# Stage 1 of a chain of weight products by six 64-column products instead of seven, and half of a side computation one iteration later

## The chip, the cores and the metric

The kernel runs on one core of a Trainium2 chip. Its time is the device time of one launch in microseconds (us); lower is better. Three runs of the kernel before gave 474.98, 475.28 and 476.53 us.

## What is computed

128 samples of 64 channels by 1024 positions pass through four modulated 1-D convolutions ("same", "upsample" with a blur behind it, "same", "downsample" with a blur ahead of it), and the input is added to the result. Each sample has weights of its own: a style vector scales the weights by input channel, and they are normalised by output channel.

```python
def _layer(x, style, w, b, mw, mb, typ):
    s = style @ mw.T + mb
    weight = SCALE * w * s[:, None, :, None]
    demod = lax.rsqrt(jnp.sum(weight * weight, axis=(2, 3)) + EPS)
    weight = weight * demod[:, :, None, None]
    ...
    elif typ == 'upsample':
        out = jax.vmap(_conv_up)(x, weight.transpose(0, 2, 1, 3)) + b[None, :, None]
        out = _blur(out, 2.0 * blur_k, (1, 1))
    ...
for i, typ in enumerate(TYPES):
    out = _layer(out, style, weights[i], biases[i], mod_w[i], mod_b[i], typ)
x = x + out
```

There is no nonlinearity between the layers, so the four layers of one sample are one linear map. The kernel first multiplies the weights of the layers together, sample by sample, and then convolves the input once with the merged weights.

## The kernel before

Samples go in fours: `q` runs from 0 to 31, and iteration `q` handles four samples, two in each half of the 128 partitions. Every matrix product works on 64x64 blocks, and four of them (two halves of the rows, two halves of the columns) stand together as one group; each of these is fp32 and appears as two instructions in the profile, so one group gives eight MATMUL instructions.

The chain of weights of a group of samples has three stages.

- **Stage 1** multiplies the last layer's three taps with the third layer's three taps. That is a product of two polynomials with three coefficients each, whose result has five blocks of 64 columns. For the first samples, and for one group more, `stage1` does it directly with nine block products. For the other 28 groups `scale3` (ScalarE) writes the last layer's taps w0, w1, w2, scaled, and the sums w0+w1 and w1+w2 (five blocks, copied from `w3x`), `stage1_a` issues three tap products into the PSUM tile `psS` and ScalarE evicts four blocks of it to the SBUF tile `S`; `stage1_b` issues two more tap products on top of what stands in PSUM, and VectorE's SCALAR_TENSOR_TENSOR (line 481) evicts those sums to `S` while it subtracts a block that ScalarE evicted. GpSimd adds two blocks of `S` (line 484). In block products this is 2+2+1 in `stage1_a` and 1+1 in `stage1_b`, seven in all. The weights of these products are `w2n`, the third layer's taps negated and their sums.
- **Stage 2** multiplies `S` with the nine blurred taps `E` into `psR`. Where `sharing(q)` holds (iterations 5 to 27), `share_sums` (VectorE, line 501) forms sums of blocks of `S` one iteration ahead, `share` multiplies them (TensorE) into unused columns of `psA`, `share_copy` (ScalarE, line 529) copies those to `psR`, and `stage2_rest` adds the rest.
- **Stage 3** multiplies the result `R` with the first layer's taps into `W`, from which VectorE forms the combinations `H`.

The convolution (`product`, line 803) streams 340 columns per MATMUL: `conv3`, `conv1`, `conv2` and `conv0` accumulate in `psA`, `conv4` in `Y`. VectorE forms their inputs `T` from the samples `X` through `G` (`in_g2`, `in_g01` at line 712, `in04` at line 790, `in3` at line 761), GpSimd forms two of them (lines 776 and 781), and `sum1` and `sum2` on VectorE carry partial sums; `conv4` of an iteration waits for `sum2`.

The order of instructions on each engine is written out by hand: `early_turn` for iterations 0 to 3, `turn_of` for 4 to 28, and the last ones apart. `psS` and `psR` share one buffer (`ps_w` has one), so `share_copy` can write only when VectorE's eviction of `S` has read `psS`. The rows' ends are computed apart from the convolution, and that work is put into single iterations by the tables `SIDE`, `LATE` and `SLOTS`: `side(SIDE, q)` stands on VectorE between `in_g2` and the eviction of `S`, `side(LATE, q)` after `in3`. `setup1(0)` and `setup1(1)` blur the second layer's taps for the row ends, two VectorE instructions each; `ends1`, a product in iteration 14, reads their result.

## Time and profile before

| what | before |
|---|---|
| runs (us) | 474.98, 475.28, 476.53; median 475.28 |
| the profiled execution: its span (us), the one time that the profile gives for it | 475.5 |
| granted TensorE clock, mean | 0.998 |
| TensorE busy (us, share of the span) | 469.7 (99%) |
| VectorE busy | 417.3 (88%) |
| ScalarE busy | 312.0 (66%) |
| GpSimd busy | 165.8 (35%) |
| data moved, mean rate | 70.71 MB, 149 GB/s |

The page lists, for each engine, the time in which it was busy. PE is TensorE's matmuls, PEld its weight loads, DVE VectorE, ACT ScalarE, POOL GpSimd, SP the queue that issues most DMAs. In the timeline each row is a run of like instructions: the start in us, the time from the first start to the last end, the engine, the line of the kernel, the operation, the tiles written and read, the shapes and the count, and in brackets the engine's idle time before it with what ended it. Because matmuls overlap, the time that a run of them takes of the engine is read from its start to the start of the next run.

### The profile page before, as it was taken

What the parts mean: (1) busy time and instruction counts of PE and PEld (TensorE: products, weight loads), DVE (VectorE), ACT (ScalarE), POOL (GpSimd) and SP (SyncE); (2) the same over time, 40 slices, a digit from 0 to 9 for tenths busy, and PEclk for the clock granted to TensorE, in tenths of its full rate; (3) what the DMA queues carried; (4) which work ended last, traced back from release to release, by engine and by line L of the source; (5) the groups of instructions that cost most, each with busy time, mean ns of one, the idle gap of its engine ahead of it and who ended that gap; (6) DMA issues with size and microseconds to landing.
All of it is one profiled execution on the core that took longest, in us unless ns stands there. A gap on an engine that the chain in (4) does not pass through costs nothing.

```text
span 475.5 us, 26771 instructions
## 1 busy us (share of the span) xinstructions
PE 469.7 (99%) x11932; PEld 349.5 (74%) x11932; DVE 417.3 (88%) x694; ACT 312.0 (66%) x711; POOL 165.8 (35%) x200
## 2 busy tenths in 40 slices
PE   9999999999999999999999999999999999999996
PEld 6987788777678876677776677766788787876653
DVE  3889998879989998899979899979998999999896
ACT  4565657577766676766667666667666777766464
POOL 3634033664444342233432233422333423243200
PEclk9999999999999999999999999999999999999999
DMA  5237456535445554345544454543555544455225
GB/s 176 71 115 224 150 151 180 152 113 177 139 145 166 166 166 136 123 150 169 163 150 126 130 168 152 178 124 121 152 164 169 164 145 147 148 152 161 80 91 193
DMA packets 52707, 70.71 MB, mean 149 GB/s; under 512 B 6000, under 2 KB 50672, under 8 KB 52592
## 3 DMA queue, kind: packets, MB, share of 16 engines
q1 hardware_dynamic: 52368, 68.78, 46.3%
q8 instruction: 93, 1.52, 1.4%
q10 hardware_dynamic: 224, 0.22, 0.1%
q14 instruction: 22, 0.18, 0.1%
HBM read 35.36 MB, written 33.62 MB: 145 GB/s over the span
## 4 chain that ended last, share of the span: by engine, by line
PE 99%; DVE 0%; ACT 0%; issue 0%
PE psA L803 47%; PE Y L803 12%; PE psR L506 9%; PE psW L621 7%; PE psA L621 7%; PE psS L428 6%; PE psR L589 5%; PE psA L506 2%; PE Y L1044 2%; PE Y L183 1%; PE Y L379 1%; PE psM L220 0%; PE psE L1044 0%; PE Y L255 0%; DVE o L882 0%; PE psM L255 0%
## 5 line engine op out<-in xcount | busy, mean ns | idle before, releaser
L803 PE MATMUL psA<-T,H 64*64 64x340 f32 x2304 | 185.9, 446 | 0.0
L803 PEld LDWEIGHTS psA<-T,H 64*64 64x64 f32 x2304 | 90.7, 133 | 46.9 <-issue 2.5
L712 DVE SCALAR_TENSOR_TENSOR G<-X 128x1376 f32<-128x1376 f32 (+2 forms) x65 | 78.0, 1206 | 0.2
L776 POOL TENSOR_TENSOR T<-G 128x684 f32<-128x684 f32 x28 | 46.3, 1652 | 73.7 <-DVE G L712 73.7
L484 POOL TENSOR_TENSOR S<-S 128x128 f32<-128x128 f32 x28 | 21.6, 772 | 139.7 <-ACT S L399 139.6
L399 ACT ACTIVATE R<-psR,tC 128x448 f32<-128x448 f32 x63 | 36.6, 631 | 43.6 <-PE psR L506 25.8
L803 PE MATMUL psA<-T,Wf 64*64 64x340 f32 x768 | 63.7, 446 | 0.0
L803 PE MATMUL Y<-T,Wf 64*64 64x340 f32 x768 | 62.4, 451 | 0.0
L712 DVE SCALAR_TENSOR_TENSOR Y<-m,psA 128x340 f32<-128x340 f32 x62 | 32.0, 516 | 28.2 <-PE psA L803 26.9
L399 ACT ACTIVATE psW<-psA 128x128 f32<-128x128 f32 x100 | 19.3, 268 | 49.1 <-PE psA L621 45.0
L790 DVE TENSOR_TENSOR T<-G 128x1368 f32<-128x1368 f32 (+1 forms) x33 | 50.8, 1541 | 0.0
L399 ACT ACTIVATE Wf<-psW,t 128x256 f32<-128x256 f32 (+2 forms) x76 | 32.7, 480 | 26.7 <-PE psW L621 26.4
L761 DVE TENSOR_TENSOR T<-X 128x684 f32<-128x684 f32 x32 | 47.7, 1492 | 0.0
L506 PE MATMUL psR<-S,E 64*64 64x64 f32 (+1 forms) x1472 | 46.8, 237 | 0.0
L781 POOL TENSOR_TENSOR T<-G 128x684 f32<-128x684 f32 x28 | 46.5, 1660 | 0.0
L428 PEld LDWEIGHTS psS<-wd,w2n 64*64 64x64 f32 x1120 | 35.1, 133 | 12.9 <-issue 0.3
L506 PEld LDWEIGHTS psR<-S,E 64*64 64x64 f32 x1472 | 39.5, 134 | 4.9 <-ACT psR L529 0.2
L803 PEld LDWEIGHTS Y<-T,Wf 64*64 64x64 f32 x768 | 30.3, 132 | 16.8
L803 PEld LDWEIGHTS psA<-T,Wf 64*64 64x64 f32 x768 | 29.8, 133 | 14.5
L880 ACT ACTIVATE o<-psA,tb,td 128x340 f32<-128x340 f32 x63 | 37.1, 648 | 5.0 <-PE psA L803 2.8
L880 ACT ACTIVATE o<-y,tb,td 128x340 f32<-128x340 f32 x62 | 38.5, 678 | 0.0
L880 ACT ACTIVATE o<-Y,tb,td 128x340 f32<-128x340 f32 x62 | 36.1, 639 | 2.8 <-PE Y L803 2.0
(180 smaller groups left out, 840.4 us busy)
## 6 DMA issues: line engine op xcount, KB each, us to landing
out<-o SPq DMA_DIRECT2D x191, 170.0 KB, 2.6
X<-in_x SPq DMA_DIRECT2D x150, 172.0 KB, 3.4
X<-in_x SPq DMA_DIRECT2D x14, 516.0 KB, 5.0
par<-in_params SPq DMA_DIRECT2D x3, 192.0 KB, 3.8
Xe<-in_x_ends SPq DMA_DIRECT2D x1, 512.0 KB, 4.5
out<-Oe SPq DMA_DIRECT2D x2, 96.0 KB, 2.1
out<-o ACTq DMA_DIRECT2D x1, 170.0 KB, 2.8
par<-in_params SPq DMA_DIRECT2D x1, 160.0 KB, 2.7
```

The source lines that it names most:

```text
L399: nc_a.activation(dst, src, AF.Copy, scale=f)
L428: nc.tensor.matmul(ps[r][cols, at * C : (at + n) * C], weight[rows], wd[c if r == 0 else 1 - c][rows, taps], start=first, stop=last, skip_ ...
L506: nc.tensor.matmul(dst[r][cols], weight[rows], st[c if r == 0 else 1 - c][rows, slots, :], start=False, stop=last, skip_group_check=True,)
L589: nc.tensor.matmul(ps[r][cols, lo * C : (lo + m) * C], E[rows, e + 2, :], src[rows, a, :], start=(n == 0), stop=(n == 8), skip_group_check ...
L621: nc.tensor.matmul(dst[r][cols], weight[rows], t[rows, c, slots, :], start=first, stop=last, skip_group_check=True,)
L712: nc_v.scalar_tensor_tensor(out, x, f, y, op0=ALU.mult, op1=op)
L761: nc_v.tensor_sub(t[:, pairs, 0, :NJ], plane(X, 3, pairs), plane(X, 1, pairs))
L776: eng.tensor_add(t[:, :, 0, :NJ], plane(g, 2), plane(g, 1))
L781: eng.tensor_sub(t[:, :, 1, :NJ], plane(g, 2), plane(g, 1))
L790: nc_v.tensor_sub(t[:, pairs, :, :NJ], both(a, PL), both(b, 1))
L803: nc.tensor.matmul(ps[s][cols, :NB], w, Ts[q, tag][rows, c, i, g : g + NB], start=(g == 0 and (m == 3 or alone)), stop=(g == K - 1), skip_ ...
L880: nc_a.activation(dst, src, AF.Identity, bias=add, scale=d3)
```

## The change

Stage 1 of the 28 groups of samples uses another identity for the same product: six block products p0, p2, p1 of single taps and three products of sums, (w0+w1), (w1+w2) and (w0+w2), each 64 columns wide. `w3x`, `w2n` and `wd` get a sixth block, w0+w2, which two more GpSimd additions fill once; `scale3` copies 384 columns instead of 320. `stage1_a` issues the three single products and `stage1_b` the three products of sums. ScalarE evicts with four instructions of 128 columns instead of two of 256: p0 and p2 for each half, then p1 for each half, written twice. GpSimd now has two instructions, an addition and a subtraction, and they stand in `stage1_a` ahead of VectorE's eviction, which reads what they write; before, one addition stood in `stage1_b` behind it in the code. VectorE's two evictions have 192 columns instead of 128 and write the three middle blocks of `S`. The blocks of `S` lie in another order, so the slices of stage 2 and of `share_sums` are other ones; the number and the widths of their products are the same. `stage1`, the direct form, has three tap products of 192 columns instead of three of 128 and three of 64. Last, `setup1(1)` moves from `LATE` at iteration 13 to `SIDE` at iteration 14.

```diff
 def split_weights():
     nc_g.tensor_copy(w3x[:, :K], w3)
     nc_g.tensor_scalar_mul(w2n[:, :K], woi[2], -1.0)
     for t, src in ((w3x, w3), (w2n, woi[2])):
-        nc_g.tensor_add(t[:, K:], src[:, : K - 1], src[:, 1:])
+        nc_g.tensor_add(t[:, K : K + 2], src[:, : K - 1], src[:, 1:])
+        nc_g.tensor_add(t[:, K + 2], src[:, 0], src[:, 2])
...
 def stage1(q, pool=None, engs=(nc_a, nc_a), between=None):
-    for k, (at, at1) in enumerate(((0, 3), (3, 1), (1, 4))):
-        tap_matmul(ps, wd, at, 2, woi[2][:, k, :], EVEN, first=k == 0)
-        tap_matmul(ps, wd, at1, 1, woi[2][:, k, :], slice(1, 2), last=k == K - 1)
+    for k in range(K):
+        tap_matmul(ps, wd, k, K, woi[2][:, k, :], slice(0, K), first=k == 0, last=k == K - 1)
...
 def stage1_a(q, ps=None):
-    tap_matmul(ps, wd, 2, 2, w2n[:, 0, :], EVEN, first=True)
-    tap_matmul(ps, wd, 3, 2, w2n[:, 2, :], EVEN)
-    tap_matmul(ps, wd, 1, 1, w2n[:, 1, :], slice(1, 2))
+    for n, (i, at) in enumerate(((0, 1), (2, 3), (1, 4))):
+        tap_matmul(ps, wd, at, 1, w2n[:, i, :], slice(i, i + 1), first=n == 0)
     st, t = s_tiles(q)
     for r in range(2):
-        scaled_copy(nc_a, flat(st[r][:, :4]), ps[r][:, C : 5 * C], tBn[:, q, r : r + 1])
+        ends = ps[r][:, C : 5 * C].rearrange("c (a b o) -> c a b o", a=2, b=2)[:, :, 0]
+        scaled_copy(nc_a, st[r][:, 0:5:4, :], ends, tBn[:, q, r : r + 1])
+    for r in range(2):
+        middle = ps[r][:, None, 4 * C : 5 * C].to_broadcast([P, 2, C])
+        scaled_copy(nc_a, st[r][:, 5:8:2, :], middle, tBn[:, q, r : r + 1])
+    nc_g.tensor_add(t[:, :, 6], t[:, :, 0], t[:, :, 4])
+    nc_g.tensor_sub(t[:, :, 6], t[:, :, 6], t[:, :, 5])
...
 def stage1_b(q):
-    tap_matmul(ps, wd, 2, 1, w2n[:, 3, :], slice(3, 4))
-    tap_matmul(ps, wd, 4, 1, w2n[:, 4, :], slice(4, 5), last=True)
+    for n, (i, at) in enumerate(((3, 1), (4, 3), (5, 2))):
+        tap_matmul(ps, wd, at, 1, w2n[:, i, :], slice(i, i + 1), last=n == K - 1)
     for r in range(2):
-        p1 = st[r][:, 0:1, :].to_broadcast([P, 2, C])
-        sums = ps[r][:, 2 * C : 6 * C].rearrange("c (a b o) -> c a b o", a=2, b=2)[:, :, 0]
         nc_v.scalar_tensor_tensor(
-            st[r][:, 4:6, :], sums, tB[:, q, r : r + 1], p1, op0=ALU.mult, op1=ALU.subtract
+            flat(st[r][:, 1:4]),
+            ps[r][:, C : 4 * C],
+            tB[:, q, r : r + 1],
+            flat(st[r][:, 5:8]),
+            op0=ALU.mult,
+            op1=ALU.subtract,
         )
-    nc_g.tensor_add(t[:, :, 2], t[:, :, 2], t[:, :, 0])
...
 def stage2_taps(q, taps, ps):
         if e % 2 == 0:
-            a, lo, m = slice(1, 4), e // 2 + 1, 3
+            a, lo, m = slice(0, 5, 2), e // 2 + 1, 3
         else:
-            a, lo, m = slice(4, 6), (e + 3) // 2, 2
+            a, lo, m = slice(1, 4, 2), (e + 3) // 2, 2
...
 SIDE = {
     13: lambda: setup1(0),
+    14: lambda: setup1(1),
...
-LATE = {13: lambda: setup1(1)}
```

GpSimd's queue around iteration 13, where stage 1 makes `S17`. Before (`T12` and `R16` are the inputs of the convolution and the sums for stage 3):

```order
L781 TENSOR_TENSOR T12_14_4066<-G14_3999 128x2x342
L484 TENSOR_TENSOR S17_4261<-S17_4261 128x2x64
L776 TENSOR_TENSOR T12_15_4339<-G15_4269 128x2x342
L638 TENSOR_TENSOR R16_4401<-R16_4401 128x2x128
L781 TENSOR_TENSOR T12_15_4339<-G15_4269 128x2x342
```

The same place in the changed kernel:

```order
L786 TENSOR_TENSOR T12_14_4111<-G14_4041 128x2x342
L472 TENSOR_TENSOR S17_4306<-S17_4306 128x2x64
L473 TENSOR_TENSOR S17_4306<-S17_4306 128x2x64
L781 TENSOR_TENSOR T12_15_4389<-G15_4318 128x2x342
L643 TENSOR_TENSOR R16_4451<-R16_4451 128x2x128
L786 TENSOR_TENSOR T12_15_4389<-G15_4318 128x2x342
```

One instruction on `S17` became two, at the same place in the queue.

VectorE's queue in iteration 13 before (`g1` is written by `setup1`, `Y` by `sum2` of the next iteration):

```order
L501 TENSOR_TENSOR S16_3991<-S16_3991 128x2x128
L712 SCALAR_TENSOR_TENSOR G15_4269<-X1_106 128x2x342
L1016 SCALAR_TENSOR_TENSOR g1_159<-par_97,g1_159 128x192 x2
L481 SCALAR_TENSOR_TENSOR S17_4261<-psS17_0_4247,tB_132,S17_4261 128x128
L481 SCALAR_TENSOR_TENSOR S17_4261<-psS17_1_4248,tB_132,S17_4261 128x128
L712 SCALAR_TENSOR_TENSOR G15_4269<-X1_106 128x2x688
L712 SCALAR_TENSOR_TENSOR y1_14_4333<-psA14_4154,m3_14_4264 128x680
L761 TENSOR_TENSOR T3_15_4335<-X1_106 128x2x342
L1016 SCALAR_TENSOR_TENSOR g1_159<-par_97,g1_159 128x192 x2
L712 SCALAR_TENSOR_TENSOR Y_119<-m3_14_4264,psA14_4154 128x340 x2
```

The same place in the changed kernel:

```order
L506 TENSOR_TENSOR S16_4029<-S16_4029 128x2x128
L717 SCALAR_TENSOR_TENSOR G15_4318<-X1_106 128x2x342
L1021 SCALAR_TENSOR_TENSOR g1_159<-par_97,g1_159 128x192 x2
L482 SCALAR_TENSOR_TENSOR S17_4306<-psS17_0_4292,tB_132,S17_4306 128x192
L482 SCALAR_TENSOR_TENSOR S17_4306<-psS17_1_4293,tB_132,S17_4306 128x192
L717 SCALAR_TENSOR_TENSOR G15_4318<-X1_106 128x2x688
L717 SCALAR_TENSOR_TENSOR y1_14_4385<-psA14_4199,m3_14_4313 128x680
L766 TENSOR_TENSOR T3_15_4387<-X1_106 128x2x342
L717 SCALAR_TENSOR_TENSOR Y_119<-m3_14_4313,psA14_4199 128x340 x2
```

The second pair on `g1` no longer stands between `T3` and `Y`, and the two evictions of `S17` are wider. The pair now stands in the next iteration, ahead of the eviction of `S18`, in the changed kernel:

```order
L506 TENSOR_TENSOR S17_4306<-S17_4306 128x2x128
L717 SCALAR_TENSOR_TENSOR G16_4596<-X0_105 128x2x342
L1021 SCALAR_TENSOR_TENSOR g1_159<-par_97,g1_159 128x192 x2
L482 SCALAR_TENSOR_TENSOR S18_4584<-psS18_0_4570,tB_132,S18_4584 128x192
L482 SCALAR_TENSOR_TENSOR S18_4584<-psS18_1_4571,tB_132,S18_4584 128x192
L717 SCALAR_TENSOR_TENSOR G16_4596<-X0_105 128x2x688
```

In the kernel before, the evictions of `S18` follow `G16` directly.

More of the change, by code (lines that the diff above doesn't have):

```diff
@@ L401, in scaled_copy @@
             eng.tensor_scalar(dst, src, f, None, op0=ALU.mult)
-    w3x = const.tile([P, 5, C], F32, name="w3x")
-    w2n = const.tile([P, 5, C], F32, name="w2n")
+    w3x = const.tile([P, 6, C], F32, name="w3x")
+    w2n = const.tile([P, 6, C], F32, name="w2n")
     def split_weights():
@@ L456, in stage1 @@
         for r in range(2):
[L457 removed]
+            scaled_copy(engs[r], flat(st[r][:, :5]), ps[r][:, : 5 * C], tB[:, q, r : r + 1])
         chain[q] = st
@@ L500, in share_sums @@
         t = whole[q]
-        nc_v.tensor_add(t[:, :, 6:8], t[:, :, 1:5:3], t[:, :, 2:6:3])
+        nc_v.tensor_add(t[:, :, 5:7], t[:, :, 0:2], t[:, :, 2:4])
     def chain_matmul(dst, weight, st, slots, last=False):
@@ L518, in share @@
         p12, p34 = ([b[:, i:j] for b in ps] for i, j in zip(at, at[1:]))
-        chain_matmul(p12, E[:, 2], chain[q], slice(6, 7))
-        chain_matmul(p34, E[:, 6], chain[q], slice(6, 7))
-        chain_matmul(p34, E[:, 5], chain[q], slice(7, 8), True)
+        chain_matmul(p12, E[:, 2], chain[q], slice(5, 6))
+        chain_matmul(p34, E[:, 6], chain[q], slice(5, 6))
+        chain_matmul(p34, E[:, 5], chain[q], slice(6, 7), True)
         shared_ps[q] = [b[:, at[0] : at[2]] for b in ps]
@@ L540, in stage2_rest @@
         plan = (
[L541 removed]
+            (apart, E[:, 0], slice(0, 5, 4)),
             (block(1), Ed[:, 0], slice(2, 3)),
[L543 to L544 removed]
+            (block(2), Ed[:, 1], slice(0, 1)),
+            (block(3), E[:, 2], slice(4, 5)),
             (block(3), Ed[:, 2], slice(2, 3)),
[L546 to L554 removed]
+            (block(4), Ed[:, 3], slice(0, 1)),
+            (block(4), E[:, 4], slice(4, 5)),
+            (block(5, 2), E[:, 8], slice(2, 5, 2)),
+            (block(5), E[:, 6], slice(4, 5)),
+            (block(1, 2), E[:, 1], slice(1, 4, 2)),
+            (block(2), E[:, 3], slice(1, 2)),
+            (block(3), Ed[:, 4], slice(3, 4)),
+            (block(4), Ed[:, 5], slice(1, 2)),
+            (block(5), E[:, 7], slice(3, 4)),
         )
@@ L1547, in turn_of @@
         in3(c)
-        side(LATE, q)
         if s == NQ:
```

16 lines of the change are left out of this document (1 added, 15 removed).

## Prediction

> **What bounds the kernel now.** I read the page first, for the busy shares and the chain that ended last.
>
> ```profile
> PE 469.7 (99%) x11932; PEld 349.5 (74%) x11932; DVE 417.3 (88%) x694; ACT 312.0 (66%) x711; POOL 165.8 (35%) x200
> ...
> PEclk9999999999999999999999999999999999999999
> ...
> PE 99%; DVE 0%; ACT 0%; issue 0%
> ```
>
> TensorE is busy for 99% of the span, at full granted clock, and 99% of the last chain is TensorE following TensorE. So its work counts one for one, and any new wait of TensorE counts one for one too. Next the timeline of one ordinary iteration, 12.
>
> ```profile
> 210.53 0.73 PE L428 MATMUL psS<-wd,w2n 64*64 64x128 f32 x24
> ...
> 211.08 1.90 PE L803 MATMUL psA<-T,Wf 64*64 64x340 f32 x24
> 211.29 0.84 ACT L399 ACTIVATE S<-psS,tBn 128x256 f32<-128x256 f32 x2 [0.32 <-PE psS L428]
> 211.53 0.42 DVE L501 TENSOR_TENSOR S<-S 128x256 f32<-128x256 f32 x1
> 211.86 0.87 DVE L712 SCALAR_TENSOR_TENSOR G<-X 128x684 f32<-128x684 f32 x1
> ...
> 212.21 0.82 POOL L484 TENSOR_TENSOR S<-S 128x128 f32<-128x128 f32 x1 [5.16 <-ACT S L399]
> ...
> 212.64 0.81 DVE L1066 TENSOR_TENSOR Ye<-Ye,c 128x384 f32<-128x384 f32 x1
> 212.80 0.41 PE L428 MATMUL psS<-wd,w2n 64*64 64x64 f32 x16
> ...
> 213.03 0.53 PE L506 MATMUL psA<-S,E 64*64 64x64 f32 x24
> ...
> 213.38 0.60 DVE L481 SCALAR_TENSOR_TENSOR S<-psS,tB,S 128x128 f32<-128x128 f32 x2
> 213.38 1.90 PE L803 MATMUL psA<-T,H 64*64 64x340 f32 x24
> 213.80 0.63 ACT L529 COPY psR<-psA 128x256 f32<-128x256 f32 x2
> ...
> 215.10 0.40 PE L506 MATMUL psR<-S,E 64*64 64x128 f32 x8
> ```
>
> TensorE's runs follow start to start without a hole. The other engines work in its shadow: ScalarE evicts `S`, GpSimd adds, VectorE evicts the sums, ScalarE copies the shared products to `psR` (213.80 to 214.43), and TensorE uses them at 215.10, 0.67 us later. That margin is what the change can use up.
>
> **TensorE's part.** The 24 instructions of `stage1_a` take 211.08 − 210.53 = 0.55 us, the 16 of `stage1_b` 213.03 − 212.80 = 0.23 us: 0.78 us. The next run, 24 instructions of 64 columns, takes 213.38 − 213.03 = 0.35 us, 14.6 ns each. Six products of 64 columns are 2 × 24 such instructions: 0.70 us. That saves 0.08 us, or 0.09 before rounding (a seventh of the columns, less the cost of eight more instructions). There are 28 groups (56 evictions by ScalarE below, two each): 28 × 0.085 = **2.4 us**. The four direct `stage1` lose instructions but no column; under 0.1 us together, counted at 0.05. Stage 2 has the same products from other places of `S`.
>
> One rule speaks against this. The Trainium skill's page "TensorE: Matmul & The Clock Gate", in its section "Wait — 56ns, not 53.3ns?", says that matmuls never start less than about 25 ns apart, however few columns they have. By it, as an estimate, 48 narrow ones would take 1.2 us and the iteration would lose 0.2 us or more where I count a gain. The rows above, 16 in 0.23 us, show that the floor does not hold for these quarter-array products, and the sum goes by the rows.
>
> **The evictions.** Their prices, by form:
>
> ```profile
> L481 DVE SCALAR_TENSOR_TENSOR S<-psS,tB,S 128x128 f32<-128x128 f32 x56 | 16.7, 339 | 2.6 <-PE psS L428 1.3 <-ACT o L880 1.0
> ...
> L712 DVE SCALAR_TENSOR_TENSOR H<-H,Wf 128x384 f32<-128x384 f32 x64 | 35.7, 558 | 2.1
> ```
>
> ```profile
> L399 ACT ACTIVATE S<-psS,tBn 128x256 f32<-128x256 f32 x56 | 23.5, 471 | 11.6 <-PE psS L428 11.6
> ...
> L399 ACT ACTIVATE Wf<-psW,t 128x192 f32<-128x192 f32 x13 | 4.8, 419 | 0.6 <-PE psW L621 0.5 <-PE Y L964 0.2
> ```
>
> VectorE: 339 ns for 128 columns, 558 for 384, so some 0.39 us for 192; both together 0.70 instead of 0.60 us, **0.10 later**. ScalarE: 471 ns for 256, 419 for 192, so some 0.37 for 128; like the pair above (0.84 us for two of 0.47) they overlap by 0.10, so four take 0.37 + 3 × 0.27 = 1.16 us instead of 0.84. `stage1_a` is 24 × 14.6 ns = 0.35 us long, not 0.55, so they start 0.20 earlier, at 211.09, and end at 212.25; `stage1_b` would start at 212.60, so TensorE doesn't wait for them. `scale3` has 64 columns more, 0.05 us each; ScalarE has slack for both.
>
> **GpSimd's pair** is the risk, because VectorE's eviction now waits for it.
>
> ```profile
> L484 POOL TENSOR_TENSOR S<-S x28: 455/821/1622, 40.6 to 426.5; 128x128 f32<-128x128 f32 x28
> ```
>
> ```profile
> 356.34 0.87 DVE L712 SCALAR_TENSOR_TENSOR G<-X 128x684 f32<-128x684 f32 x1
> ...
> 357.05 0.47 POOL L484 TENSOR_TENSOR S<-S 128x128 f32<-128x128 f32 x1 [5.50 <-ACT S L399]
> 357.12 1.02 DVE L1130 TENSOR_TENSOR Ue<-Ve 128x576 f32<-128x576 f32 x1
> ```
>
> Its addition takes 0.46 us alone, 0.82 in the middle. In iteration 12 it ended (213.03) 0.30 after VectorE's `G` (212.73), in iteration 22 0.31 after it (357.52, 357.21): it sits out the running `G` and then goes ahead of VectorE's next instruction. That one pays some 0.25 us: `Ye` took 0.81 for the 384 columns for which `H` takes 0.56. In the changed kernel the addition needs only the first two evictions: it is ready at 211.09 + 0.27 + 0.37 + 0.07 = 211.80, in time (it needs its operands 0.16 after its start) for the gap between `S` (ends 211.95) and `G`. Then `G` is pushed by 0.25, the subtraction follows in the gap behind `G`, and the evictions of `S` start at about 213.40 where VectorE has no side work, as now, but 0.25 later where it has. With the 0.10, and TensorE arriving 0.09 earlier, the copies to `psR` eat **0.44 us** of their margin in iterations with side work, 0.2 in the others. The margins run from 0.67 down to these two, iterations 17 and 18:
>
> ```profile
> 286.25 0.61 DVE L481 SCALAR_TENSOR_TENSOR S<-psS,tB,S 128x128 f32<-128x128 f32 x2
> 286.69 0.63 ACT L529 COPY psR<-psA 128x256 f32<-128x256 f32 x2 [0.24 <-DVE S L481]
> ...
> 287.67 0.40 PE L506 MATMUL psR<-S,E 64*64 64x128 f32 x8
> ```
>
> ```profile
> 300.92 0.63 ACT L529 COPY psR<-psA 128x256 f32<-128x256 f32 x2 [0.62 <-DVE S L481]
> ...
> 301.33 0.41 PEld L506 LDWEIGHTS psR<-S,E 64*64 64x64 f32 x6 [0.23 <-ACT psR L529]
> ```
>
> Iteration 17 has 0.35 (0.30 with 0.05 for the signal), so 0.14 of wait; in iteration 18 TensorE waits already, so all 0.44; some others are just touched, 0.1 in sum: **0.7 us**, from 0 (the pair costs VectorE nothing) to about 2 (below).
>
> **The early iterations.** Stage 2 of groups 3 and 4 reads an `S` that was evicted just before:
>
> ```profile
> 42.87 0.60 DVE L481 SCALAR_TENSOR_TENSOR S<-psS,tB,S 128x128 f32<-128x128 f32 x2
> 44.89 1.05 DVE L712 SCALAR_TENSOR_TENSOR Y<-m,psA 128x340 f32<-128x340 f32 x2
> ```
>
> ```profile
> 43.35 2.91 PE L589 MATMUL psR<-S,E 64*64 64x192 f32 x72
> 45.99 0.56 PE L803 MATMUL Y<-T,Wf 64*64 64x340 f32 x4
> ```
>
> VectorE's eviction (to 43.47) sets when half of `psR` can start, and `Y` (to 45.94) when `conv4` can. So the gain of two iterations is not had (0.17) and 0.10 is added: **0.25 us**, up to 0.6 if GpSimd pushes VectorE here too; nothing if the other half hides it. The two additions that fill `w0+w2` lie at 18 to 22 us ahead of an idle GpSimd and cost nothing.
>
> **The moved pair.** After it, in iteration 13, VectorE was nearly late for `sum2`:
>
> ```profile
> 232.36 0.36 DVE L1016 SCALAR_TENSOR_TENSOR g<-par,g 128x192 f32<-128x192 f32 x1
> ...
> 232.84 0.52 DVE L712 SCALAR_TENSOR_TENSOR Y<-m,psA 128x340 f32<-128x340 f32 x1
> ```
>
> ```profile
> DVE Y L712 <- PE psA L803: 26.9, 26, 1.9
> ```
>
> 0.12 us of slack stood there, against 1.0 on average (26.9 in 26). The change frees some 0.8 there, which covers the 0.44 that VectorE now loses, and puts it into iteration 14, whose `psR` waits for a row-end product of TensorE as well. I count it at nothing; left in place it would have cost about 0.4.
>
> **The sum** against the profiled span of 475.5 us: −2.4 − 0.05 + 0.25 + 0.7 = **−1.5**, 474.0. The median of the runs, 475.28, lies 0.2 below the span; by it the changed kernel takes 473.8, and I say 473.9. A measurement of this kernel tells 0.3% from no change, 1.4 us: the line lies at 473.85, on my forecast.
>
> **Rivals.**
>
> *The addition misses its gap.* It is ready 0.15 us ahead of the end of `S` and needs 0.16: the closest race in the sum. The row of iteration 22 (ready 0.16 before `G` ended, and first) speaks for it. If it loses, it sits out `G`, ends at 213.03 as now, and the subtraction sits out VectorE's side work; the evictions of `S` come 0.43 later where that is one long instruction. Then the margin eaten is 0.62, and sixteen iterations wait between 0 and 0.45 us, 2.1 in all: −2.4 − 0.05 + 0.25 + 2.1 = −0.1, 475.2, no change. The Trainium skill's page "GPSIMD Engine Reference", section "8. Key points", says that GpSimd shares its SBUF interfaces with VectorE and contends with VectorE instructions that have two SBUF inputs; `S`, `G` and the side work have two, and the rows above agree (0.46 alone, 0.82 beside `G`).
>
> *The pair is slow everywhere.* If each of the two takes the 0.82 us of the median row and they start behind `G`, the pair ends at 213.35 to 213.9, the evictions come some 0.6 later in all iterations, and 0.79 is eaten from margins of 0.35 to 0.67: 0.15 to 0.8 us in each of 23 iterations, 5.6 in all. −2.2 + 5.6 = +3.4, 478.7, slower. It decides once the waits add up to more than 2.4 us, an eaten margin of about 0.64. Against it: alone the addition takes 0.46, and VectorE idles ahead of the eviction where it has no side work.
>
> *The pair costs VectorE nothing*: the waits are 0 to 0.2 and the time is 472.9. Against it stands the row of `Ye`.
>
> *The narrow matmuls cost more than they save*, a floor of 27 ns on every instruction (the price of 128 columns: 0.55 us less 8 × 14.6 ns, by 16): 48 × 27 = 1.3 us, +0.5 each, +14 in all, 489. The 16 in 0.23 us rule it out but for surprises.
>
> **How the numbers follow.** Forecast 0.46, missed gap 0.31, slow pair 0.11, free pair 0.10, floor 0.02. The forecast's own bounds (early cost 0 to 0.6, waits 0.3 to 1.2) run from 473.2 to 474.6 and split at the line: 0.28 faster, 0.18 same. With the free pair faster has 0.10 more and 0.02 from the missed gap: 0.40. Same: 0.18 + 0.28 = 0.46. Slower: 0.11 + 0.02 + 0.01 = 0.14. The range takes in the free pair and the missed gap with its bounds: 472.8 to 476.0.
>
> **What would show it.** Right: 24 and 24 narrow instructions of stage 1 take 0.35 us each; GpSimd's addition starts near 1.27 us after `stage1_a` and `G` starts 0.25 later than now; the copies to `psR` end some 0.3 later in iterations with side work, and TensorE's wait for them appears in iterations 17 and 18. Wrong: a wait of TensorE for `psR` in most iterations (missed gap or slow pair), a wait of `conv4` for `sum2`, or 48 narrow instructions taking over 0.78 us.

## The result and the profile after

| kernel | median (us) | lowest to highest | runs |
|---|---|---|---|
| before, beside after | 475.98 | 474.98 to 477.19 | 10 |
| after | 477.63 | 476.05 to 478.43 | 10 |

The ratio of after to before is 1.0031, 95% interval 1.0016 to 1.0046: slower by about 1.5 us (the medians differ by 1.65). Forecast were 473.9 us, 1.4 below the kernel before, and a range of 472.8 to 476.0; both are missed. Of the 3.7 us between forecast and result, 0.7 is the baseline: the three runs ahead of the prediction had a median of 475.28, the ten beside after one of 475.98. A second set of runs of the same kernel gave 477.18 us, ratio 1.0023 (1.0009 to 1.0036).

The page of after shows the same bound and more work on the other engines: VectorE 427.3 us instead of 417.3, GpSimd 182.6 instead of 165.8. TensorE has 128 more instructions and is busy for 2 us less; the last chain is TensorE's as far back as it could be followed, 48% of the span.

```profile
PE 467.7 (99%) x12060; PEld 346.5 (73%) x12060; DVE 427.3 (90%) x694; ACT 324.2 (68%) x767; POOL 182.6 (38%) x230
```

Iteration 12, in the timeline of after, has what the prediction asked for:

```profile
208.87 0.53 PE L429 MATMUL psS<-wd,w2n 64*64 64x64 f32 x24
209.22 1.90 PE L808 MATMUL psA<-T,Wf 64*64 64x340 f32 x24
...
209.43 1.14 ACT L399 ACTIVATE S<-psS,tBn 128x128 f32<-128x128 f32 x4
209.87 0.42 DVE L506 TENSOR_TENSOR S<-S 128x256 f32<-128x256 f32 x1
210.14 0.46 POOL L472 TENSOR_TENSOR S<-S 128x128 f32<-128x128 f32 x1 [4.74 <-ACT S L399]
210.20 1.13 DVE L717 SCALAR_TENSOR_TENSOR G<-X 128x684 f32<-128x684 f32 x1
...
210.72 0.93 POOL L473 TENSOR_TENSOR S<-S 128x128 f32<-128x128 f32 x1
...
210.94 0.53 PE L429 MATMUL psS<-wd,w2n 64*64 64x64 f32 x24
...
211.25 0.81 DVE L1071 TENSOR_TENSOR Ye<-Ye,c 128x384 f32<-128x384 f32 x1
211.28 0.53 PE L511 MATMUL psA<-S,E 64*64 64x64 f32 x24
...
211.98 0.73 DVE L482 SCALAR_TENSOR_TENSOR S<-psS,tB,S 128x192 f32<-128x192 f32 x2
```

Each half of stage 1 now takes TensorE 0.35 us (208.87 to 209.22, 210.94 to 211.28), as forecast. GpSimd's addition starts 1.27 us after `stage1_a` (210.14 − 208.87), as forecast, and wins the gap ahead of `G`. `G` then takes 1.13 us instead of 0.87, and the side work behind it pays once more (`Ye` 0.81, as before; without any pair, in no_pair below, it takes 0.55). By groups, `G` with 684 columns cost 866 ns before and 1040 after, 5.6 us more of VectorE in all. The group before comes first, then those of after, with the pair's own:

```profile
L712 DVE SCALAR_TENSOR_TENSOR G<-X 128x684 f32<-128x684 f32 x32 | 27.7, 866 | 0.2
```

```profile
L717 DVE SCALAR_TENSOR_TENSOR G<-X 128x684 f32<-128x684 f32 x32 | 33.3, 1040 | 0.2
...
L482 DVE SCALAR_TENSOR_TENSOR S<-psS,tB,S 128x192 f32<-128x192 f32 x56 | 20.4, 405 | 2.2 <-PE psS L429 1.4 <-POOL S L473 0.7
...
L472 POOL TENSOR_TENSOR S<-S 128x128 f32<-128x128 f32 x28 | 13.9, 495 | 133.5 <-ACT S L399 133.5
...
L473 POOL TENSOR_TENSOR S<-S 128x128 f32<-128x128 f32 x28 | 23.1, 823 | 3.3
...
L781 POOL TENSOR_TENSOR T<-G 128x684 f32<-128x684 f32 x28 | 46.3, 1652 | 75.9 <-DVE G L717 75.9
```

Only 0.7 us of VectorE's idle time ahead of the eviction is put down to the pair. Nor does the pair hold up GpSimd's own queue as a whole: ahead of `T<-G` GpSimd idles for 75.9 us, waiting for VectorE's `G` (73.7 before).

**How two profiles are laid side by side.** The spans of single executions don't compare: the start of the first `conv4` alone lies between 29.22 and 31.42 us in the profiles below. So I read the start of `conv4` (the first row of `Y<-T,Wf`) in each iteration and compare the steps from one to the next. For iterations 14 and 15, after and then the second profile of before:

```profile
232.52 1.95 PE L808 MATMUL Y<-T,Wf 64*64 64x340 f32 x24
...
248.71 1.95 PE L808 MATMUL Y<-T,Wf 64*64 64x340 f32 x24
```

```profile
233.69 1.95 PE L803 MATMUL Y<-T,Wf 64*64 64x340 f32 x24
...
249.25 1.95 PE L803 MATMUL Y<-T,Wf 64*64 64x340 f32 x24
```

The step 14 to 15 takes 16.19 us after and 15.56 before: +0.63. All steps against that second profile of before, in us:

| step | after | after, second profile | no pair in groups 8 to 30 (off_pair) | split_sums |
|---|---|---|---|---|
| plain ones (6, 9, 11, 19, each to the next) | −0.08 to −0.09 | −0.08 to −0.09 | −0.08 to −0.09 | −0.02 to −0.09 |
| 0 to 1 | +0.13 | +0.11 | −0.07 | −0.07 |
| 3 to 4 | +0.46 | +0.44 | +0.22 | +0.23 |
| 4 to 5 | +0.49 | +0.48 | +0.43 | +0.20 |
| 13 to 14 | +0.31 | −0.14 | +0.19 | −0.09 |
| 14 to 15 | +0.63 | +0.62 | +0.16 | −0.09 |
| 18 to 19 | +0.37 | +0.37 | −0.09 | +0.04 |
| 21 to 22 | +0.09 | +0.38 | +0.38 | −0.11 |
| all, from conv4 of iteration 0 to the end | +1.61 | +1.25 | −0.19 | −0.39 |

So the gain on TensorE is there, 28 × 0.09 = 2.5 us, and more than that is lost, at a few places that come again in both profiles of after, and in smaller waits that don't.

### The profile page after: what moved, and what is told of

Same layout as the page of the kernel before. It is cut to its first block, busy times and chain, and to the rows that moved or that the text cites. A ratio compares the mean times of both kernels' runs of the same rounds, so it can differ in the third digit from the quotient of the medians.

```text
span 474.3 us, 27139 instructions
## 1 busy us (share of the span) xinstructions
PE 467.7 (99%) x12060; PEld 346.5 (73%) x12060; DVE 427.3 (90%) x694; ACT 324.2 (68%) x767; POOL 182.6 (38%) x230
## 5 line engine op out<-in xcount | busy, mean ns | idle before, releaser
L808 PEld LDWEIGHTS psA<-T,H 64*64 64x64 f32 x2304 | 92.0, 133 | 47.0 <-issue 2.9
L717 DVE SCALAR_TENSOR_TENSOR G<-X 128x1376 f32<-128x1376 f32 (+2 forms) x65 | 83.7, 1295 | 0.2
L781 POOL TENSOR_TENSOR T<-G 128x684 f32<-128x684 f32 x28 | 46.3, 1652 | 75.9 <-DVE G L717 75.9
L472 POOL TENSOR_TENSOR S<-S 128x128 f32<-128x128 f32 x28 | 13.9, 495 | 133.5 <-ACT S L399 133.5
L511 PE MATMUL psR<-S,E 64*64 64x64 f32 (+1 forms) x1472 | 47.8, 238 | 0.0
L511 PEld LDWEIGHTS psR<-S,E 64*64 64x64 f32 x1472 | 41.1, 134 | 4.9 <-ACT psR L534 0.9
L808 PEld LDWEIGHTS Y<-T,Wf 64*64 64x64 f32 x768 | 29.3, 132 | 17.9
L429 PEld LDWEIGHTS psS<-wd,w2n 64*64 64x64 f32 x1344 | 32.8, 134 | 12.6 <-issue 0.2
```

Source lines behind the costliest of these rows:

```text
L429: nc.tensor.matmul(ps[r][cols, at * C : (at + n) * C], weight[rows], wd[c if r == 0 else 1 - c][rows, taps], start=first, stop=last, skip_ ...
L472: nc_g.tensor_add(t[:, :, 6], t[:, :, 0], t[:, :, 4])
L511: nc.tensor.matmul(dst[r][cols], weight[rows], st[c if r == 0 else 1 - c][rows, slots, :], start=False, stop=last, skip_group_check=True,)
L717: nc_v.scalar_tensor_tensor(out, x, f, y, op0=ALU.mult, op1=op)
L781: eng.tensor_add(t[:, :, 0, :NJ], plane(g, 2), plane(g, 1))
L808: nc.tensor.matmul(ps[s][cols, :NB], w, Ts[q, tag][rows, c, i, g : g + NB], start=(g == 0 and (m == 3 or alone)), stop=(g == K - 1), skip_ ...
```

## The experiments

Theory A says that a few waits, each with its own cause, ate the gain; theory B that GpSimd's pair is the price, and then whether by VectorE's wait for it or by its contention with VectorE. The table gives the medians and the ratios to before; the text then takes the kernels in groups.

| kernel | median (us) | ratio to before (95%) |
|---|---|---|
| after_again | 477.18 | 1.0023 (1.0009 to 1.0036) |
| before_again | 476.32 | 0.9996 (0.9980 to 1.0011) |
| move_only | 476.52 | 1.0008 (0.9995 to 1.0020) |
| move_back | 478.23 | 1.0048 (1.0023 to 1.0072) |
| g_first | 476.47 | 1.0011 (0.9997 to 1.0025) |
| no_pair | 475.45 | 0.9987 (0.9968 to 1.0005) |
| pair_unwaited | 477.16 | 1.0027 (1.0010 to 1.0043) |
| one_add | 475.53 | 0.9990 (0.9975 to 1.0005) |
| off_pair | 474.75 | 0.9973 (0.9957 to 0.9990) |
| before_no_add | 477.11 | 1.0027 (1.0012 to 1.0042) |
| add_once | 475.62 | 0.9991 (0.9977 to 1.0005) |
| off_pair2 | 476.04 | 1.0007 (0.9994 to 1.0019) |
| off_pair3 | 475.94 | 1.0002 (0.9989 to 1.0015) |
| memset_late | 476.70 | 1.0024 (1.0008 to 1.0039) |
| split_sums | 474.85 | 0.9978 (0.9963 to 0.9992) |

### Second profiles of both kernels

after_again and before_again have no edit.

> The changed kernel unchanged, for a second profile. Theory A (few exposed waits: TensorE has its 2.4 us, and three or four places in iterations 3, 4, 14 and 18 eat them): the starts of conv4, laid beside those of the kernel before, lose again about 0.9 us in all between iterations 3 and 5 and 0.6 from 14 to 15, and gain 0.06 to 0.12 in plain iterations; from conv4 of iteration 0 to the end about +0.7 us against before. Theory B (the pair on GpSimd): what varies is how often the addition misses its gap: more than three additions of over 0.8 us, each with a loss of 0.2 to 0.6 in its own iteration, and a span of 475.5 or more.

> The kernel before unchanged, for a second profile, since the first one was of an execution near the slowest of its runs. If that profile had waits that the program does not need: the steps from conv4 of iteration 2 to 3, 21 to 22 and 31 to the end are shorter by 0.35 to 0.4, 0.2 to 0.4 and 0.1 to 0.3 us, and from conv4 of iteration 0 to the end some 0.8 us less than in the first. If the first was typical: within 0.2 us.

The losses of after come again to 0.02 us at 0 to 1, 3 to 4, 4 to 5, 14 to 15 and 18 to 19; those at 13 to 14 and 21 to 22 don't. In the second profile of before the steps 2 to 3, 21 to 22, 25 to 26 and 31 to the end are 0.42, 0.33, 0.14 and 0.16 us shorter than in the first, and the whole from `conv4` of iteration 0 on is 0.87 shorter. The profile on which the prediction was worked out had thus 0.9 us of waits that the program does not need; against the second one after loses 1.25 to 1.61 us, which is what the ratios say (1.1 and 1.5). From the first profile alone it would have been 0.4 to 0.7.

### The moved pair

move_only:

```diff
+        14: lambda: setup1(1),
...
-    LATE = {13: lambda: setup1(1)}
...
-        side(LATE, q)
```

> The kernel before with nothing changed but the place of setup1(1): from behind in3 in iteration 13 to ahead of the eviction of S in iteration 14. Theory A: TensorE waits for g ahead of ends1 in iteration 14, 0.4 to 0.7 us, against some 0.1 to 0.3 that iteration 13 gains: +0.2 to +0.6 us against before. Theory B: the move is free by itself, the product finds g ready, within 0.1 us of before by the starts of conv4.

move_back:

```diff
-        14: lambda: setup1(1),
...
+    LATE = {13: lambda: setup1(1)}
...
         in3(c)
+        side(LATE, q)
```

> The changed kernel with setup1(1) back behind in3 in iteration 13. Theory A: the wait for g in iteration 14 is gone (0.66 us), conv4 of iteration 13 waits up to 0.4 for sum2: -0.2 to -0.6 us against the changed kernel. Theory B: no difference over 0.1 us, since the eviction of S behind it still waits for the pair.

g_first:

```diff
+        if q == 14:
+            side(SIDE, q)
         in_g2(c)
-        side(SIDE, q)
+        if q != 14:
+            side(SIDE, q)
```

> The changed kernel with setup1(1) still in iteration 14, but ahead of G on VectorE instead of behind it. If the wait of ends1 is the place behind G: g is ready some 0.9 us earlier, before ends1 is due, the step from conv4 of 14 to 15 loses 0.0 to 0.1 in place of 0.62 us against the kernel before, the eviction of S is no earlier, all other steps stay: -0.5 us against the changed kernel. If the lateness of VectorE as a whole is the cause (psR waits there next): 0.3 us or more of the loss stays.

In after, TensorE waits for `g`, with `ends1` and everything behind it:

```profile
238.09 1.14 DVE L717 SCALAR_TENSOR_TENSOR G<-X 128x684 f32<-128x684 f32 x1
...
239.15 1.00 DVE L1021 SCALAR_TENSOR_TENSOR g<-par,g 128x192 f32<-128x192 f32 x2
239.19 0.53 PE L511 MATMUL psA<-S,E 64*64 64x64 f32 x24
240.06 0.74 DVE L482 SCALAR_TENSOR_TENSOR S<-psS,tB,S 128x192 f32<-128x192 f32 x2
...
240.20 1.96 PE L1049 MATMUL Y<-Ye,g 64*64 64x384 f32 x24 [0.48 <-DVE g L1021]
```

`ends1` was due at 239.54 (239.19 and 0.35 for 24 narrow instructions) and starts at 240.20. With `g` ahead of `G` (g_first) it starts without a wait, although `g` itself takes longer there, and `S` is evicted hardly earlier (0.81 us after `share`'s start, as against 0.87):

```profile
239.82 1.21 DVE L1021 SCALAR_TENSOR_TENSOR g<-par,g 128x192 f32<-128x192 f32 x2
...
240.93 0.53 PE L511 MATMUL psA<-S,E 64*64 64x64 f32 x24
240.96 0.86 DVE L717 SCALAR_TENSOR_TENSOR G<-X 128x684 f32<-128x684 f32 x1
...
241.28 1.91 PE L1049 MATMUL Y<-Ye,g 64*64 64x384 f32 x24
...
241.74 0.73 DVE L482 SCALAR_TENSOR_TENSOR S<-psS,tB,S 128x192 f32<-128x192 f32 x2
```

The step goes from +0.62 to −0.09: with the place behind `G` the whole loss of 0.71 us is gone; the medians differ by 0.1 to 0.2% in the same direction, which alone would prove little. The place and GpSimd act together here: with seven products and the one addition of the kernel before, move_only has +0.37 in that step, and after without the pair (no_pair, below) +0.09. The median of move_only, +0.08%, is not told from none, and its profile has 0.70 us in the step 6 to 7 that no other profile has. Left behind `in3` in iteration 13 of the changed kernel (move_back), the pair meets something worse:

```profile
231.22 0.72 POOL L643 TENSOR_TENSOR R<-R 128x256 f32<-128x256 f32 x1 [0.62 <-ACT R L399]
231.25 2.62 DVE L1021 SCALAR_TENSOR_TENSOR g<-par,g 128x192 f32<-128x192 f32 x2
...
231.91 1.75 POOL L786 TENSOR_TENSOR T<-G 128x684 f32<-128x684 f32 x1
...
233.79 1.05 DVE L717 SCALAR_TENSOR_TENSOR Y<-m,psA 128x340 f32<-128x340 f32 x2
...
234.90 1.95 PE L808 MATMUL Y<-T,Wf 64*64 64x340 f32 x24 [1.90 <-DVE Y L717]
```

The two `g` take 2.62 us where they took 0.70 before: GpSimd's `R` and `T<-G` were there first, and each `g` ends some 0.2 us behind GpSimd's instruction. `conv4` waits 1.90 us, the step 13 to 14 is 2.04 longer. I had expected −0.2 to −0.6 us against after; it was +1.5 to +1.9 from `conv4` of iteration 0 on in the profiles, and about +1 by the ratios, so the change is better with its move than without it.

### GpSimd's pair: wait or contention

no_pair:

```diff
-            middle = ps[r][:, None, 4 * C : 5 * C].to_broadcast([P, 2, C])
-            scaled_copy(nc_a, st[r][:, 5:8:2, :], middle, tBn[:, q, r : r + 1])
-        nc_g.tensor_add(t[:, :, 6], t[:, :, 0], t[:, :, 4])
-        nc_g.tensor_sub(t[:, :, 6], t[:, :, 6], t[:, :, 5])
+            middle = ps[r][:, None, 4 * C : 5 * C].to_broadcast([P, 3, C])
+            scaled_copy(nc_a, st[r][:, 5:8, :], middle, tBn[:, q, r : r + 1])
```

> The changed kernel without GpSimd's addition and subtraction; ScalarE writes the block p1 three times instead of twice (its middle evictions have 192 columns), so that the middle block of S lacks p0 + p2. Theory A: G starts 0.25 earlier again and the evictions of S come earlier, but only the waits for psR in iterations 13 to 18 go: -0.4 to -0.8 us against the changed kernel; the losses of iterations 3, 4 and 14 stay. Theory B: the pair is the price of the change: -1.5 us or more against the changed kernel, and a time below that of the kernel before.

pair_unwaited is no_pair with the pair put back on a ninth block:

```diff
+        nc_g.tensor_add(t[:, :, 8], t[:, :, 0], t[:, :, 4])
+        nc_g.tensor_sub(t[:, :, 8], t[:, :, 8], t[:, :, 5])
```

> The changed kernel with GpSimd's addition and subtraction kept, on the same data and at the same place, but writing to a ninth block of S that nobody reads; VectorE's eviction subtracts the block p1, which ScalarE writes three times (so the middle block of S lacks p0 + p2). It tells the wait for the pair from the contention with it. Wait theory: VectorE evicts S as soon as its side work ends, the losses at 14 to 15 and 18 to 19 go, -1.0 us or more against the changed kernel. Contention theory: G and the side work are still pushed by 0.25 and 0.25 us, and at most 0.5 us of the 1.8 that leaving out the pair brought comes back.

one_add:

```diff
-        for n, (i, at) in enumerate(((0, 1), (2, 3), (1, 4))):
+        for n, (i, at) in enumerate(((0, 1), (2, 3))):
             tap_matmul(ps, wd, at, 1, w2n[:, i, :], slice(i, i + 1), first=n == 0)
+        tap_matmul(ps, wd, 2, 1, woi[2][:, 1, :], slice(1, 2))
...
-            middle = ps[r][:, None, 4 * C : 5 * C].to_broadcast([P, 2, C])
-            scaled_copy(nc_a, st[r][:, 5:8:2, :], middle, tBn[:, q, r : r + 1])
+            middle = ps[r][:, None, 2 * C : 3 * C].to_broadcast([P, 2, C])
+            scaled_copy(nc_a, st[r][:, 5:8:2, :], middle, tB[:, q, r : r + 1])
...
-        nc_g.tensor_sub(t[:, :, 6], t[:, :, 6], t[:, :, 5])
```

> The same six products with one GpSimd instruction instead of two and the whole result: p1 is made with its positive weight and put into the middle block of psS, where the third product of sums lands on it, so that VectorE has to subtract p0 + p2 alone. Wait theory: the subtraction, the later of the two, is what VectorE waits for; without it the loss at 14 to 15 is under 0.3 us and that at 18 to 19 near 0: -0.7 to -1.2 us against the changed kernel, about the time of the kernel before. Contention theory: half of the contention stays: -0.4 to -0.9.

off_pair is one_add, and for groups 8 to 30 the following (with other slices where the blocks of `S` are written and read):

```diff
-        nc_g.tensor_add(t[:, :, 6], t[:, :, 0], t[:, :, 4])
+        if not sharing(q - 3):
+            nc_g.tensor_add(t[:, :, 6], t[:, :, 0], t[:, :, 4])
...
-        nc_v.tensor_add(t[:, :, 5:7], t[:, :, 0:2], t[:, :, 2:4])
+        nc_v.tensor_add(t[:, :, 2], t[:, :, 1], t[:, :, 7])
+        nc_v.tensor_sub(t[:, :, 3], t[:, :, 4], t[:, :, 0])
```

> One step on from the last: in the 23 groups with shared products GpSimd does nothing for S. VectorE subtracts p2 in place of p0 + p2 in the middle block, which gives S0 + S2 at once, the sum that the shared products need; one iteration later it adds S1 + S3 and forms S2 by subtracting S0 (two instructions of 128 columns, some 0.33 us each, in place of one of 256, 0.42). The whole result. If the six products are worth their 2.4 us and GpSimd was their price: from conv4 of iteration 0 on 1.2 to 2 us less than the changed kernel, 474.5 to 475.5, below the kernel before. If TensorE's gain does not turn into time because other engines are due at the same points: within 0.5 us of the kernel before.

The expectations of one_add and off_pair call their result whole, but it isn't: in neither does a product of stage 1 write the fourth block of `psS`, onto which the copied sums of the shared products go later. off_pair2 and split_sums below, which put a product there, compute the whole result. Instructions and sizes are as described, and the times are read for that.

pair_unwaited decides between wait and contention. VectorE no longer waits for the pair, yet nothing is gained: 1.0027, between the two measurements of after, and the steps 14 to 15 and 18 to 19 keep their +0.63 and +0.38. Its iteration 12 reads like that of after:

```profile
210.93 0.47 POOL L472 TENSOR_TENSOR S<-S 128x128 f32<-128x128 f32 x1 [4.73 <-ACT S L399]
211.00 1.13 DVE L717 SCALAR_TENSOR_TENSOR G<-X 128x684 f32<-128x684 f32 x1
...
211.62 0.83 POOL L473 TENSOR_TENSOR S<-S 128x128 f32<-128x128 f32 x1 [0.22 <-ACT S L399]
...
212.05 0.81 DVE L1071 TENSOR_TENSOR Ye<-Ye,c 128x384 f32<-128x384 f32 x1
...
212.79 0.73 DVE L482 SCALAR_TENSOR_TENSOR S<-psS,tB,S 128x192 f32<-128x192 f32 x2
```

Without the pair (no_pair) the time falls by 0.36% of ratio, 1.7 us, `Ye` takes 0.55 us instead of 0.81, and TensorE no longer waits for `g`. In iteration 18 the weights of stage 2 wait for ScalarE's copy to `psR`, here in after:

```profile
301.12 0.41 PEld L511 LDWEIGHTS psR<-S,E 64*64 64x64 f32 x6 [0.64 <-ACT psR L534]
```

The same wait is 0.65 us in pair_unwaited, 0.39 in one_add and 0.13 in no_pair; before it was 0.23. So what the pair costs, it costs by contention, not by the wait.

With one instruction instead of two (one_add) the time falls by about as much as without both, although `G` stays pushed (1034 ns on average). That is more than the 0.4 to 0.9 us that contention was expected to give back; in the profiles, from `conv4` of iteration 0 on, it is 0.4 to 0.8. With none in 23 groups (off_pair) the ratio is 0.9973, below before, as forecast, and the steps 0 to 1 and 18 to 19 have −0.07 and −0.09. One push seems to cost little by itself: the kernel before has one too (its addition pushes the side work, as `Ye` to 0.81), and leaving out nearly all of its additions brings nothing (add_once, below).

What stays open: the profiles of no_pair and one_add are 1.48 and 0.84 us longer than that of before_again from `conv4` of iteration 0 on, while their medians are below before (both intervals take in 1). 1.30 of no_pair's 1.48 is one collision, described next; single profiles carry scattered waits of the size of the rest, and I have only one of each.

### What GpSimd's absence does to the kernel before

before_no_add and add_once:

```diff
-        nc_g.tensor_add(t[:, :, 2], t[:, :, 2], t[:, :, 0])
```

```diff
+        if q == 7:
+            nc_g.tensor_add(t[:, :, 2], t[:, :, 2], t[:, :, 0])
```

> The kernel before without its one GpSimd addition (so the middle block of S lacks p0). It tells whether the gain without the pair comes from the six products or from GpSimd being away. Six products: the kernel before has margin for its addition, 0 to -0.3 us against it. Contention theory: VectorE is what bounds, and the 0.25 us in 28 iterations brings -0.5 us or more here too.

> The kernel before with its GpSimd addition left in for group 7 alone (iteration 3), so that the middle block of S lacks p0 elsewhere. Without any addition the kernel before became slower by 1.2 us: GpSimd's T<-G of iteration 3 started 2.1 us earlier and VectorE's small oc, 0.235 us otherwise, took 1.308 behind it. If that collision is all of it, T<-G starts behind the one addition again, oc takes 0.235, and the time is that of the kernel before or up to 0.4 below it. If the additions themselves are worth something (or their absence costs), the 1.2 us stay or half of them.

Taking the one addition out of the kernel before makes it 0.27% slower, against both theories. Its step 3 to 4 is 1.07 us longer, and iteration 3 shows why:

```profile
83.90 1.70 POOL L775 TENSOR_TENSOR T<-G 128x684 f32<-128x684 f32 x1 [10.00 <-PE psA L802]
...
84.11 0.17 DVE L975 TENSOR_TENSOR oc<-Y,dm 128x16 f32<-128x16 f32 x1
...
84.33 1.31 DVE L976 TENSOR_SCALAR oc<-oc,par_s 128x16 f32<-128x16 f32 x1
...
85.55 0.85 DVE L711 SCALAR_TENSOR_TENSOR y<-psA,m 128x680 f32<-128x680 f32 x1
...
86.55 0.80 PE L802 MATMUL psA<-T,H 64*64 64x340 f32 x8 [0.98 <-DVE y L711]
```

With the addition left in for that one group, `T<-G` starts long after `oc`, and the time is 0.9991:

```profile
83.87 0.23 DVE L978 TENSOR_SCALAR oc<-oc,par_s 128x16 f32<-128x16 f32 x1
...
85.49 0.45 POOL L485 TENSOR_TENSOR S<-S 128x128 f32<-128x128 f32 x1 [12.03 <-ACT S L399]
...
85.91 1.65 POOL L777 TENSOR_TENSOR T<-G 128x684 f32<-128x684 f32 x1
```

The addition stands ahead of `T<-G` in GpSimd's queue and waits for ScalarE's `S` until 85.49, and so holds `T<-G` back past `oc`. no_pair has the same collision in its profile (+1.30 in that step). What the other 27 additions cost the kernel before can't be told from nothing (0.9991, 0.9977 to 1.0005).

### The early iterations, and a version that beats both

off_pair2 puts p2 into the fourth block for groups 8 to 31 and pays for it on VectorE:

```diff
-        for n, (i, at) in enumerate(((0, 1), (2, 3))):
+        for n, (i, at) in enumerate(((0, 1), (2, 4 if own else 3))):
...
+        nc_v.tensor_sub(t[:, :, 3:8:4], t[:, :, 4:8:3], t[:, :, 0:7:6])
+        nc_v.tensor_add(t[:, :, 2], t[:, :, 1], t[:, :, 7])
```

> The version without GpSimd once more, with the product p2 alone in the fourth block of psS (the copied sums of the shared products need that all four blocks have been written by a product), so that VectorE's blocks are S1, S0 + S2 and S3 + S4; one iteration later one subtraction of 256 columns gives S2 and S3 (0.42 us) and one addition of 128 columns S1 + S3 (0.33). The whole result, for groups 8 to 31. Theory that contention with GpSimd was the price of the six products: 0.09 us more of VectorE in each iteration than in the run before, still no wait of TensorE in iterations 14 and 18; 474.5 to 475.2, 0.7 to 1.4 below the kernel before. Rival, VectorE's time itself is the price: 0.33 us more than in the changed kernel's share_sums, within 0.3 us of the kernel before or above it.

off_pair3 adds:

```diff
         stage2(c)
+        if q == FIRST + 1:
+            small(FIRST)
...
-        if q in SMALL:
+        if q in SMALL and not entry:
             small(q)
```

> The same, and the small product of iteration 4 (Y from c0f and wsum) issued behind the next stage 2, so that TensorE doesn't wait for VectorE's memset of Y, which waits for ScalarE's output copy, which stands behind the four evictions of S. If that queue is the loss from 4 to 5: 0.2 to 0.35 us less between conv4 of iteration 4 and conv4 of iteration 5 than in the kernel it is made from, the rest unchanged. If not, the loss stays at 0.4 to 0.5.

memset_late is the changed kernel with the edit of off_pair3 and:

```diff
+        if not entry:
+            clear()
...
             stage1_b(s)
+        if entry:
+            clear()
         in_g01(c)
```

where `clear` holds the memset of `Y`.

> The changed kernel with VectorE's memset of Y in iteration 4 behind the eviction of S instead of ahead of it, and the small product that needs it behind the next stage 2. If stage 2 of iteration 5 waits for S, and S for that memset (which waits for ScalarE's output copy behind the four evictions of S): the step from conv4 of 4 to 5 loses 0.0 to 0.2 us in place of 0.5, the rest stays: -0.3 to -0.5 us against the changed kernel. If it is the copy m alone, 0.4 or more stays.

off_pair2 missed its expectation: 1.0007, no gain, with +0.44 in the step 14 to 15. Ahead of the eviction VectorE has two instructions of 355 ns on average where after has one of 418; in off_pair they are two of 285, and off_pair does gain. That these 0.3 us are the price fits the rival in the expectation, but no run shows it by itself. Moving the small product alone did nothing (4 to 5 stays at +0.42). Moving the memset as well took that step of the changed kernel from +0.48 to +0.20. In after the order is visible: the memset waits 2.26 us for ScalarE's `o`, behind the four evictions, and holds the eviction of `S`, whose buffer stage 2's `psR` needs:

```profile
98.22 1.19 ACT L885 ACTIVATE o<-Y,tb,td 128x340 f32<-128x340 f32 x2
...
99.50 0.14 DVE L1528 MEMSET Y<- 128x96 f32 x1 [2.26 <-ACT o L885]
99.55 0.72 DVE L482 SCALAR_TENSOR_TENSOR S<-psS,tB,S 128x192 f32<-128x192 f32 x2
```

memset_late's median, 1.0024, shows no gain: 0.28 us is below what one set of runs tells.

split_sums keeps p1 in the fourth block, and VectorE subtracts p1, p2 and p1; both edits above are in it too:

```diff
-        nc_v.tensor_add(t[:, :, 5:7], t[:, :, 0:2], t[:, :, 2:4])
+        nc_v.tensor_add(t[:, :, 4:6], t[:, :, 1:3], t[:, :, 3:8:4])
+    def own_block(q):
+        t = whole[q]
+        nc_v.tensor_sub(t[:, :, 2], t[:, :, 5], t[:, :, 0])
...
             stage1_b(s)
+        if sharing(q):
+            own_block(c + 1)
```

> Six products with neither GpSimd nor a longer VectorE chain ahead of the eviction of S: VectorE subtracts p2 in the middle block, adds S1 + S3 and the block + p1 = S0 + S2 in one instruction of 256 columns as in the kernel before, and forms S2 by one subtraction of 128 columns behind the eviction (groups 8 to 30); the early groups have the single addition, and both of the edits above are in. The whole result. If contention and these two places were all that ate the 2.4 us: from conv4 of iteration 0 to the end 0.7 to 1.4 us less than the second profile of the kernel before, 474.8 to 475.5. If VectorE's lateness moves to sum2 (0.33 us more ahead of Y, whose slack is 0.4 to 0.8): waits of conv4 for Y appear in several iterations, and the time is that of the kernel before.

It computes the whole result in 474.85 us: 0.9978 of before (0.9963 to 0.9992), about 1 us faster, and 0.5% faster than the change. `G` is back at 877 ns, the added subtraction costs 281 ns behind the eviction, and no wait for `Y` appears:

```profile
L728 DVE SCALAR_TENSOR_TENSOR G<-X 128x684 f32<-128x684 f32 x32 | 28.1, 877 | 0.3
...
L517 DVE TENSOR_TENSOR S<-S 128x128 f32<-128x128 f32 x23 | 6.5, 281 | 0.0
```

The time is as forecast, but from `conv4` of iteration 0 to the end it is 0.39 us below the second profile of before, not the 0.7 to 1.4 expected. So contention and the two places don't account for all that is lost: the steps 3 to 4, 4 to 5 and 15 to 16 still have +0.23, +0.20 and +0.31.

## Why the prediction was wrong, step by step

Three terms failed. The moved pair, counted at nothing, cost 0.7 us; the early iterations, 0.25 in the sum, cost 1.3; and the waits, 0.7 in the sum, came to 1.8 to 2.1. Together they are more than TensorE's gain, which was right.

**TensorE's part**, −2.4: right. 0.09 us in each plain step, 2.5 in 28. The floor on narrow instructions did not show (24 in 0.35 us).

**The evictions** and **GpSimd's pair**, as durations: right. 405 ns each for VectorE's (0.39 forecast), 0.73 to 0.74 us for two; 1.14 for ScalarE's four (1.16 forecast); the addition ready at 1.27 us, `G` pushed by 0.26. That `Ye` pays some 0.25 was read from a different instruction, `H`, and was right as well: 0.55 alone.

**The early iterations**, 0.25: right where it looked (0 to 1: +0.13 where a plain step gains 0.09, so 0.22, gone in off_pair) and blind elsewhere. The steps 3 to 4 and 4 to 5 lose 0.55 and 0.58 against a plain step. In iteration 3 VectorE runs without a gap up to `y`, for which `conv2` waits:

```profile
73.38 0.38 POOL L932 TENSOR_TENSOR a<-sc 128x96 f32<-128x96 f32 x1
73.40 0.78 DVE L717 SCALAR_TENSOR_TENSOR H<-Wf 128x384 f32<-128x384 f32 x1
...
83.95 0.86 DVE L717 SCALAR_TENSOR_TENSOR y<-psA,m 128x680 f32<-128x680 f32 x1
...
84.96 0.80 PE L808 MATMUL psA<-T,H 64*64 64x340 f32 x8 [0.37 <-DVE y L717]
```

GpSimd's `a` meets `H`, which takes 0.78 instead of 0.55 (in off_pair it takes 0.55), and that goes straight to `y`. Half of the step, 0.22, stays even with a single addition: VectorE bounds there, and TensorE's gain is not had. In iteration 4 the memset, above, is 0.28 of the loss; the cause of the rest is open. The step that failed is the sentence "TensorE is busy for 99% of the span … its work counts one for one": it held in the plain steps, and I applied it to those, too, where VectorE or ScalarE is due at the same moment.

**The moved pair**, "I count it at nothing": failed, 0.71 us, shown by g_first and again by move_back, where the step 14 to 15 has −0.09. I had looked at what waits for VectorE in iteration 13, and at `psR` in 14, not at the product that reads `g` itself, which stands on TensorE right behind `share`. "Left in place it would have cost about 0.4" was wrong too, 2.04 in the one profile.

**The waits for `psR`**, 0.7 from 0 to about 2: mis-sized. The largest was priced right: iteration 18, 0.44 in the sum, costs 0.46 against a plain step. All the rest (16 to 17: 0.19; 24 to 25: 0.17; 13 to 14, 15 to 16 and 21 to 22: 0 to 0.47, not in both profiles; smaller ones) is 1.30 to 1.60 by subtraction, where the sum had 0.24; so 1.8 to 2.1 in all, at the upper bound. Not all of it is for `psR`: ahead of TensorE's holes in 15 to 16 and 21 to 22 the profiles name no other engine, and the first profile of before lost 0.33 in 21 to 22 as well. With it: −2.5 + 0.2 + 1.1 + 0.7 + 1.8 to 2.1 = +1.3 to +1.6, the difference from which the rest was taken.

**The rivals.** The slow side had 0.14, for one mechanism: a pair slow everywhere. The pair was not slow everywhere (495 and 823 ns), and a missed gap was rare: 2 of the 28 additions took over 0.8 us. The pushes were those of the forecast; what went wrong is what they cost, and two places that no rival named. The free pair, 472.9 and so 2.4 below the median by the prediction, has its nearest run in off_pair: 0.27%, 1.3 us.

**The baseline.** I laid the span of 475.5 beside the median of 475.28 as if they were one measure. A run's time is its span and some 1.8 us (after: 474.3 and 476.05), so that profile was, as an estimate, of an execution of about 477.2, near the slowest. This did not make the sum wrong, but its slack and its waits were read from an untypical execution.

## What to carry to other kernels

When GpSimd and VectorE share work, price an instruction of GpSimd by what it does to VectorE's neighbours, not by whether anybody waits for it; an instruction that comes 0.03 us too late (`g` behind `R` in move_back) can wait for a whole one of the other engine. For an instruction that is moved, look at its reader first, and at where that stands on its engine. And take two profiles of the kernel before, and compare them step by step from a common mark, before reading slack from either.

## What the runs showed of the hardware

- A VectorE instruction whose inputs all lie in SBUF and a TENSOR_TENSOR of GpSimd hold each other up, and the one that came first goes first. `oc<-oc`, 128x16, took 1.31 us behind `T<-G` instead of 0.23, and the two `g` of move_back 2.62 instead of 0.70. In none of the seventeen profiles does such a VectorE instruction start over 0.05 us into one of GpSimd's and end inside it. Those that do have an input in PSUM (`oc<-Y,dm` 0.17 us, `Y<-m,psA` 0.52, their usual times) or, a memset, none. The Trainium skill's page "GPSIMD Engine Reference", section "8. Key points", says that GpSimd shares its SBUF interfaces with VectorE and contends with VectorE instructions that have two SBUF inputs or are in a 2-port mode. The traces agree, and show the second one waiting for nearly all that is left of the other's instruction.
- Where GpSimd's 0.46 us instruction gets in between, VectorE's next one pays 0.26 to 0.28 us (`G` 1.13 or 1.14 instead of 0.86 or 0.87, `Ye` 0.81 instead of 0.55).
- The time up to the first `conv4` varies by 2.2 us between executions (29.22 to 31.42), more than the change is worth.
